# Joint stage and end of a two-layer MetaFormer kernel: other norm instructions, another transpose, new priorities, another plan of the end

## The chip, the core and the metric

The kernel runs on one core of one Trainium2 chip, in a single launch. The core has a matrix engine (TensorE, PE in the profile, its weight loads PEld), three engines for elementwise work (VectorE or DVE, ScalarE or ACT, GpSimd or POOL), and a queue that issues the transfers (SyncE or SP). Each runs its own instructions in the order in which the program gives them, and waits for the others through semaphores. The metric is the device time of one execution in microseconds (us), the median of three: 1247.04 us, from 1245.08 to 1249.42.

## The reference

An image of 64 x 64 tokens with 96 channels goes through two layers. Cut to what matters here:

```python
x = x + L0_conv_ref(ln_c(x))          # layer 0: scan mixer, depthwise convolution
t = t + ffn(ln_t(t), W1, b1, W2, b2)  # layer 0: MLP in fp8 (5,2) products, fp16 sums
x = x + L1_conv_ref(ln_c(x))          # layer 1: scan mixer, full 3x3 convolution
t = t + ffn(ln_t(t), ...)             # layer 1: MLP
# ffn:   h = relu(q16(q16(q8(x) @ q8(W1).T) + q8(b1)));  y = q16(q16(q8(h) @ q8(W2).T) + q8(b2))
# norms: (v - mean(v)) / sqrt(var(v) + eps), over the 96 channels of a token
# layer 1 mixer, per direction: h = exp(dt*A) * h + dt*u*B;  y += sum over 16 states of h*C
#        four directions (rows, columns, both ways), then * silu(z) @ W_out.T
```

## The kernel before, in words

The 4096 tokens are cut into 8 chunks of 512, kept in the tile `res` as 128 partitions x 4 tokens x 96 channels a chunk. Channels of the layer-1 mixer are cut into 6 groups of 32, and its 16 states into 4 sets of 4, so that 24 passes (group g, set k) fill 128 partitions each.

The run has four parts. Layer 0's mixer comes first. Then comes the **joint stage**, written by `middle`: what is left of layer 0's mixer (`mix0`, four pairs of chunks), its MLP (`mlp0`, eight chunks, with `norm` "b" before it and `norm` "c" after it), and the front of layer 1 (`compose1`, `conv_unit`, `project`) are put together into one order. A pair of chunks goes through `mix0`, `mlp0` and the images that the convolution reads (L1553); a convolution unit waits for the images of its chunks and of their neighbours. The stage ends when the last `project` has given the first step sizes to the scans. Third are the 24 **scan passes** (`scans`, the line L2003 holds every scan), with 16 scans of 2.2 to 2.3 us each, one after the other on VectorE. Fourth is the **end**: the last scans of the last pass, and all of what follows from them: the column sums (L2008), the sum over directions, times C, the fold over states into `acc`, the gate (L2359), the output product (L2367), and the MLP of layer 1 on eight chunks (`late_chunk`).

**What sets the order.** In the joint stage and in the end, no order is written by hand. Operations are added to an `Order` with an engine, an assumed cost in us, what they read and write, and which slot of which kind they need (banks, buffers). `Order.run` then walks a modelled clock: of the operations that could start first, it takes the one with the highest rank, which is the longest modelled path to the end plus a lead. `LEAD` gives leads to the parts of the joint stage, `LATE` to the chunks of the end. The engines then run in that order whatever the real durations are. Other tables say which engine takes which variant: `BY_SUMS` (which quarters of the last pass are summed on PE), `TIMES_POOL`, `ROUND_DVE`, `RELU_ACT`, `BIAS_POOL`, `LAST_POOL`.

**A norm** (`norm`, L1453 to L1475) is seven instructions: a DVE sum, a DVE subtraction of the mean, an ACT square, a second DVE sum, an ACT square root, a DVE reciprocal, a DVE product. In `mlp0` the fp8 result is cast by POOL to bf16 (L1489), transposed by PE (L1493) into half-bank slots, and copied by ACT. The MLP's second bias is added as fp32 to fp16 (L1530).

**The end.** The share of channel group 4 (rows 128 to 160 of W_out) in the layer's output is added for chunks 0 to 3 during the last passes, and for chunks 4 to 7 in the end: two kinds of PE products (L2308, the identity times `res`; L2310, four products of 32 rows) into a bank, and an ACT copy back to `res` (L2319). The quarters a = 0 and 1 go by PE sums, an ACT copy and a POOL product (L2328, L2342, L2344), a = 2 and 3 by a POOL sum and a POOL product (L2348, L2349); the backward row scan's part is multiplied on its own (L2354, on DVE for a = 1 and 2). `late_chunk` norms a chunk by two statistics instructions (L2393), a square root, a reciprocal and four products of one token each (L2401).

Of the kernel before, what the change touches and what calls it, by code (L numbers as in the profile page):

```python
# [124 lines left out]

IN_DVE, OTHERS = (), (15, 9, 9)


BY_SUMS, TIMES_POOL = (0, 1), (0, 3)
ROUND_DVE, RELU_ACT = [(2, 2), (5, 1), (5, 2), (6, 2), (7, 0)], [(0, 1), (2, 1), (5, 0), (7, 1)]  # L130
BIAS_POOL, LAST_POOL = (0, 1, 6), (0, 1, 2, 3)
LATE = (103.0, 38.0, -4.0, -6.0, -9.0, -12.0, -12.0, -13.0)


LEAD = {"compose": -5.0}
LEAD |= {("mix", s): t for s, t in enumerate((275.0, 0.0, -10.0, 10.0))}
LEAD |= {("mlp", s): t for s, t in enumerate((65.0, 50.0, 50.0, -145.0))}
LEAD |= {("conv", 0, 0): -275.0, ("conv", 0, "n"): -80.0, ("conv", 0, 1): -860.0}
LEAD |= {("conv", 4, 0): 115.0, ("conv", 4, "n"): 115.0, ("conv", 4, 1): -70.0}
LEAD |= {("project", 0, 0): 25.0, ("project", 0, 1): -45.0, ("project", 4, 0): 125.0, ("project", 4, 1): -235.0}  # L140


class Order:
# [8 lines left out]
    def __init__(self):  # L152
        self.ops, self.free, self.at, self.lead = [], {}, {}, 0.0

# [38 lines left out]
    def run(self, slack=0.0):  # L193
# [15 lines left out]
        while waiting:  # L209
# [23 lines left out]
            for key, tag in new.items():  # L233
                k = min(range(len(self.free[tag])), key=lambda k: self.free[tag][k][0])
                self.at[key] = self.free[tag].pop(k)[1]
            engines[engine] = t + cost
# [21 lines left out]
class Net:  # L258
# [835 lines left out]
    def middle(self, w, pool):  # L1094
# [27 lines left out]
        slots("bank", pb, 7, [P, CH])  # L1122
        t = pb.tile([P, 2, CH], BF16, tag="half", name="half")
        o.slots("half", [t[:, i] for i in range(2)])
        bp = back.enter_context(tc.tile_pool(name="back0", bufs=1))
        for tag, n, shape, dtype in (
            ("r", 2, [P, 2, 4], F32),
            ("nm", 4, [P, 4, 3 + CD], F32),
            ("ss", 1, [P, 4, CD], F32),
            ("x8", 2, [P, 4, CD], FP8),  # L1130
            ("xb", 2, [P, 4, CD], BF16),
# [6 lines left out]
            slots(tag, bp, n, shape, dtype)  # L1138
        spare = [t.rearrange("p a b -> p (a b)")[:, 0:CH] for t in self.diag]
# [4 lines left out]
        o.free["ss"].append((0.0, self.spare[0][:, 0 : 4 * CD].rearrange("p (j d) -> p j d", j=4)))  # L1144
# [197 lines left out]
    def mix0(self, s):  # L1342
# [92 lines left out]
        for k, c in enumerate(chunks):  # L1435
            o.add("ACT", 0.55, kept(c), r=[("oc", c)], new={("ot", c): "ot"})
            o.add("PE", 0.75, turned(c), r=[("ot", c)], new={("ob", c): "bank"})
            o.add("DVE", 1.15, added(k, c), r=[("ob", c), ("r", s)], w=[("res", c)])

    def norm(self, n, c, eps, to, engine="DVE"):  # L1440
# [5 lines left out]
        def spread(t):  # L1446
            return t.unsqueeze(2).to_broadcast([P, 4, CD])

        hold, m, xc, ss, v, r = ((k, n, c) for k in ("nm", "lm", "xc", "ss", "lv", "lr"))
        key = (to, n, c)  # L1450
        mean, dev, inv = (lambda i=i: at[hold].rearrange("p a b -> p (a b)")[:, 4 * i : 4 * i + 4] for i in range(3))
        mid = lambda: at[hold].rearrange("p a b -> p (a b)")[:, 12:].rearrange("p (j d) -> p j d", j=4)
        o.add("DVE", 0.52, lambda: keep(nc.vector.tensor_reduce(mean(), x, AX.X, ALU.add)), r=[("res", c)], new={hold: "nm"}, w=[m])  # L1453
        o.add(
            "DVE",
            0.56,
            lambda: keep(nc.vector.scalar_tensor_tensor(mid(), spread(mean()), -1.0 / CD, x, ALU.mult, ALU.add)),
            r=[m, hold, ("res", c)],
            w=[xc],
        )  # L1460
        o.add("ACT", 0.48, lambda: keep(nc.scalar.activation(at[ss], mid(), AF.Square)), r=[xc, hold], new={ss: "ss"})
        o.add("DVE", 0.52, lambda: keep(nc.vector.tensor_reduce(dev(), at[ss], AX.X, ALU.add)), r=[ss, hold], w=[v])
        o.add(
            "ACT",
            0.27,
            lambda: keep(nc.scalar.activation(dev(), dev(), AF.Sqrt, bias=eps, scale=1.0 / CD)),
            r=[hold],
            w=[v],
            table="sqrt",
        )  # L1470
        o.add("DVE", 0.17, lambda: keep(nc.vector.reciprocal(inv(), dev())), r=[v, hold], w=[r])
        o.add(
            "DVE",
            0.53,
            lambda: keep(nc.vector.tensor_tensor(at[key], mid(), spread(inv()), ALU.mult, saturate=False)),  # L1475
            r=[xc, r, hold],
            new={key: to},
        )
        return key

    def mlp0(self, c):
# [6 lines left out]
        xb, xt = ("xb", c), ("xt", c)  # L1488
        o.add("POOL", 0.6, lambda: keep(nc.gpsimd.tensor_copy(at[xb], at[x8])), r=[x8], new={xb: "xb"})  # L1489

        def turned():
            for j in range(4):
                keep(nc.tensor.transpose(at["t", c][0:CD, j * P : (j + 1) * P], at[xb][:, j, :], self.identb))  # L1493

        o.add("PE", 0.45, turned, r=[xb], new={("t", c): "half"})
        o.add("ACT", 0.55, lambda: keep(nc.scalar.copy(at[xt], at["t", c][0:CD])), r=[("t", c)], new={xt: "xt"})

# [6 lines left out]
        def relu(m):  # L1504
            h, b = ("h16", c, m), b1[:, m : m + 1]
            if m == 0:
                return lambda: keep(nc.scalar.activation(at[h], at[h], AF.Relu, bias=b))
# [5 lines left out]
        for m in range(nm):  # L1513
            o.add("PE", 0.45, up(m), r=[xt], new={("h", c, m): "bank", **({} if m else {("h8", c): "h8"})})
            o.add("ACT", 0.52, rounded(m), r=[("h", c, m)], new={("h16", c, m): "h16"})
            o.add(*(("DVE", 0.42), ("ACT", 0.65))[m == 0], relu(m), w=[("h16", c, m)])
            o.add("POOL", 0.65, small(m), r=[("h16", c, m), ("h8", c)], w=[("h8", c, m)])
# [1043 lines left out]
```

## Time and profile before

The profiled execution took 1247.49 us; its span from the first to the last instruction is 1245.7 us.

| | |
|---|---|
| median of three runs | 1247.04 us |
| profiled execution, its span | 1247.49 us, 1245.7 us |
| busy share of the span: DVE, PE, ACT, POOL | 92%, 82%, 71%, 68% |
| joint stage, from its first product to the first column scan | 104.5 to 319.5 us |
| scan passes | 319.5 to 1161.6 us |
| end, to the last VectorE instruction | 1161.6 to 1242.6 us |

In the rows of groups, the columns are: line, engine, operation, output and inputs by the program's names with their shapes, the number of instructions, their busy time in us, the mean of one in ns, and after the second bar the idle time of the engine just before them and what ended it. In the rows of windows the columns are: the stretch in us from the span's start, its length, busy time and number of instructions of each engine, the granted TensorE clock (1.00 is full), the share of the transfer engines and GB/s. A timeline row gives start, duration, engine, line, operation, and in brackets the idle time before it and its releaser.

### The profile page before, as it was taken

What the parts mean: (1) busy time and instruction counts of PE and PEld (TensorE: products, weight loads), DVE (VectorE), ACT (ScalarE), POOL (GpSimd) and SP (SyncE); (2) the same over time, 40 slices, a digit from 0 to 9 for tenths busy, and PEclk for the clock granted to TensorE, in tenths of its full rate; (3) what the DMA queues carried; (4) which work ended last, traced back from release to release, by engine and by line L of the source; (5) the groups of instructions that cost most, each with busy time, mean ns of one, the idle gap of its engine ahead of it and who ended that gap; (6) DMA issues with size and microseconds to landing.
All of it is one profiled execution on the core that took longest, in us unless ns stands there. A gap on an engine that the chain in (4) does not pass through costs nothing.

```text
span 1245.7 us, 11134 instructions
## 1 busy us (share of the span) xinstructions
PE 1025.0 (82%) x3478; PEld 417.4 (34%) x3478; DVE 1146.2 (92%) x928; ACT 886.1 (71%) x1073; POOL 849.4 (68%) x517
## 2 busy tenths in 40 slices
PE   9997899995287877787977777888778889898887
PEld 5532333331032222233322222233223444344444
DVE  7894987568989999999999999999999999999788
ACT  5582755456587878787887878788778878887535
POOL 3002665323588878888798788978888888876666
PEclk9998989896588788888888879898789999988885
DMA  2252011246844574555734575545736766432301
GB/s 75 75 163 52 1 26 43 85 164 226 271 141 139 179 253 152 178 184 184 244 96 144 203 247 175 173 129 180 238 120 199 239 189 240 148 100 75 99 1 51
DMA packets 79133, 183.15 MB, mean 147 GB/s; under 512 B 21534, under 2 KB 34936, under 8 KB 77688
## 3 DMA queue, kind: packets, MB, share of 16 engines
q1 hardware_dynamic: 78376, 182.16, 46.4%
q8 instruction: 29, 0.48, 0.2%
q14 instruction: 40, 0.33, 0.1%
q10 hardware_dynamic: 688, 0.19, 0.1%
HBM read 159.73 MB, written 21.52 MB: 145 GB/s over the span
## 4 chain that ended last, share of the span: by engine, by line
DVE 42%; PE 14%; issue 9%; ACT 6%; DMA 3%; POOL 0%; another core or an unknown queue 0%; POOLq 0%; DVEq 0%; SPq 0%; ACTq 0%
DVE h1s L2003 13%; DVE xws L2003 12%; DVE h0s L2003 7%; PE hs L2014 6%; DVE x2s L2003 3%; PE hs L2018 3%; DVE x1s L2003 3%; ACT da L1988 2%; DMA kept<-xn 2%; ACT xws L1973 2%; DVE x0s L2003 2%; PE acc L2042 1%; DMA dt<-hss 1%; DVE x0s L2401 1%; PE late L2310 1%
## 5 line engine op out<-in xcount | busy, mean ns | idle before, releaser
L2031 POOL TENSOR_TENSOR kept<-kept,kept 128x1024 f32<-128x1024 f32 x92 | 217.2, 2360 | 81.8 <-issue 40.5
L2008 POOL TENSOR_TENSOR hss<-h1s,xws 128x1024 f32<-128x1024 f32 x96 | 228.1, 2378 | 60.9 <-DVE xws L2003 57.1
L2014 PE MATMUL hs<-h0s,ident 128*128 128x512 f32 x360 | 223.3, 706 | 28.7 <-DVE h0s L2003 24.2
L1988 ACT ACTIVATE da<-dt1s,a 128x1024 f32<-128x1024 f32 x168 | 187.4, 1116 | 70.5 <-DVE xws L2003 55.0
L2003 DVE TENSOR_TENSOR_SCAN xws<-da,xws 128x1024 f32<-128x1024 f32 x96 | 222.9, 2321 | 10.6 <-ACT da L1988 10.3
L1988 ACT ACTIVATE da<-dt0s,a 128x1024 f32<-128x1024 f32 x166 | 185.1, 1115 | 40.7 <-DVE h0s L2003 16.9
L2018 PE MATMUL hs<-hss,ident 128*128 128x512 f32 x368 | 187.7, 602 | 13.9 <-POOL hss L2008 13.8
L2003 DVE TENSOR_TENSOR_SCAN h1s<-da,h1s,xws 128x1024 f32<-128x1024 f32 x72 | 168.0, 2334 | 0.3
L2042 PE MATMUL acc<-kept,fold 128*32 128x512 f32 x368 | 87.8, 689 | 69.5 <-POOL kept L2031 69.5
L2027 ACT COPY kept<-hs 128x512 f32<-128x512 f32 x184 | 106.9, 581 | 46.1 <-PE hs L2018 45.2
L2014 PEld LDWEIGHTS hs<-h0s,ident 128*128 128x128 f32 x360 | 72.9, 220 | 155.8 <-issue 83.0
L2018 PEld LDWEIGHTS hs<-hss,ident 128*128 128x128 f32 x368 | 69.7, 193 | 112.9 <-issue 79.2
L2014 PE MATMUL hs<-x0s,ident 128*128 128x512 f32 x128 | 75.1, 672 | 13.2 <-DVE x0s L2003 13.2
L2014 PE MATMUL hs<-x1s,ident 128*128 128x512 f32 x128 | 74.8, 670 | 12.2 <-DVE x1s L2003 12.2
L2014 PE MATMUL hs<-x2s,ident 128*128 128x512 f32 x120 | 70.2, 670 | 14.6 <-DVE x2s L2003 14.6
L1967 POOL TENSOR_TENSOR x1s<-x1s,dus 128x1024 f32<-128x1024 f32 x32 | 75.7, 2367 | 8.9 <-DMA x1s<-bc 8.9
L1967 POOL TENSOR_TENSOR x2s<-x2s,dus 128x1024 f32<-128x1024 f32 x32 | 75.8, 2370 | 0.4 <-DMA x2s<-bc 0.4
L2003 DVE TENSOR_TENSOR_SCAN x0s<-da,x0s 128x1024 f32<-128x1024 f32 x32 | 74.2, 2320 | 1.7 <-ACT da L1988 1.7
L2003 DVE TENSOR_TENSOR_SCAN x1s<-da,x1s 128x1024 f32<-128x1024 f32 x32 | 74.2, 2320 | 1.7 <-ACT da L1988 1.7
L2003 DVE TENSOR_TENSOR_SCAN x2s<-da,x2s 128x1024 f32<-128x1024 f32 x32 | 74.3, 2322 | 1.1 <-ACT da L1988 1.0
L1973 ACT COPY xws<-x1s 128x1024 f32<-128x1024 f32 x32 | 63.1, 1972 | 5.2 <-POOL hss L2008 5.2
L1967 POOL TENSOR_TENSOR x0s<-x0s,dus 128x1024 f32<-128x1024 f32 x28 | 66.4, 2371 | 0.0
(371 smaller groups left out, 1922.6 us busy)
## 6 DMA issues: line engine op xcount, KB each, us to landing
kept<-bc SPq DMA_DIRECT2D x92, 512.0 KB
x2s<-bc SPq DMA_DIRECT2D x32, 512.0 KB
x0s<-bc SPq DMA_DIRECT2D x28, 512.0 KB
x1s<-bc SPq DMA_DIRECT2D x28, 512.0 KB
dus<-du SPq DMA_DIRECT2D x20, 512.0 KB
dt1s<-dt SPq DMA_DIRECT2D x20, 512.0 KB
dt0s<-dt SPq DMA_DIRECT2D x20, 512.0 KB
kept<-xn SPq DMA_DIRECT2D x24, 384.0 KB
```

The source lines that it names most:

```text
L1967: keep(nc.gpsimd.tensor_tensor(x, x, du[:, part[j]], ALU.mult))
L1973: keep(copy(grid(xw)[:, w, :], cols(xs[i % 3])[:, w, :]))
L1988: keep(nc.scalar.activation(t, dts[o][:, part[j]], AF.Exp, scale=self.a6[:, g, k : k + 1]))
L2003: keep(nc.vector.tensor_tensor_scan(to, da, x, start, ALU.mult, ALU.add))
L2008: keep(nc.gpsimd.tensor_tensor(cols(hs)[:, w, :], grid(h1)[:, w, :], grid(xw)[:, w, :], ALU.add))
L2014: keep(nc.tensor.matmul(t, self.ident, x[:, chunk(m)], start=k == 0, stop=False))
L2018: keep(nc.tensor.matmul(sums[i, m], self.ident, hs[:, chunk(m)], start=False, stop=True))
L2027: keep(nc.scalar.copy(to, sums.pop((i, j * (SC // CH) + h))))
L2031: keep(nc.gpsimd.tensor_tensor(t, t, times_c_by(i, a), ALU.mult))
L2042: keep(nc.tensor.matmul(to, self.fold4, src, start=k == 0, stop=k == NK - 1))
L2310: keep(nc.tensor.matmul(o[:, j], y[:, j:CH:4], w, start=False, stop=j == 3))
L2401: keep(dve.tensor_scalar(at[x8][:, j], x[:, j], at[st][:, j, 1:2], at[sd][:, j : j + 1], ALU.subtract, ALU.mult, saturate=False))
```

## The change

In the **joint stage**, `norm` uses two statistics instructions on pairs of tokens (means and sums of squared deviations come from them), a subtraction, a square root, a reciprocal and a product: the square on ACT and both sums are gone. `mlp0` transposes the fp8 result by products with an fp8 identity (`narrow`), so POOL's cast is gone; its second bias is held in fp16. The eighth bank replaces the two half-bank slots. Ten products of the identity with itself stand ahead of the stage's first product. `LEAD` has other values, and some assumed costs are raised.

In the **end**, the products for group 4 of chunks 4 to 7 no longer go through `res`: with weights laid out in blocks for two chunks (`blocks`), they are summed into the same bank as those of group 5 (`blocked`), and one DVE addition puts both into `res` (`added`). The fourth load of `ye` moves from the end to the scan passes. Only a = 0 goes by PE sums, now with the backward scan's part in it and one DVE product; a = 1 goes as a = 2 and 3 do, and POOL multiplies the backward part of a = 2 and 3. `late_chunk` norms by a subtraction and a product, and chunk 1 by four ACT instructions. `fill` puts products without use into the gaps that the plan leaves on PE. The tables and `LATE` have other values.

```diff
-BY_SUMS, TIMES_POOL = (0, 1), (0, 3)
-ROUND_DVE, RELU_ACT = [(2, 2), (5, 1), (5, 2), (6, 2), (7, 0)], [(0, 1), (2, 1), (5, 0), (7, 1)]
-BIAS_POOL, LAST_POOL = (0, 1, 6), (0, 1, 2, 3)
-LATE = (103.0, 38.0, -4.0, -6.0, -9.0, -12.0, -12.0, -13.0)
-LEAD = {"compose": -5.0}
-LEAD |= {("mix", s): t for s, t in enumerate((275.0, 0.0, -10.0, 10.0))}
-LEAD |= {("mlp", s): t for s, t in enumerate((65.0, 50.0, 50.0, -145.0))}
+BY_SUMS, TIMES_POOL = (0,), (0, 2, 3)
+ROUND_DVE = ((0, 0), (0, 1), (1, 1), (3, 1), (6, 1), )
+RELU_ACT = ((0, 1), (1, 1), (1, 2), (4, 0), (4, 2), (5, 2), (6, 1), (7, 1), )
+NORM_ACT, BIAS_POOL, LAST_POOL = (1,), (0, 1), (0, 1, 2, 4)
+LATE = (195.0, 601.0, -262.0, -558.0, 321.0, -603.0, -581.0, 1149.0)
+LEAD = {"compose": -84.0}
+LEAD |= {("mix", s): t for s, t in enumerate((1589.0, 1847.0, -1582.0, -1562.0))}
+LEAD |= {("mlp", s): t for s, t in enumerate((1510.0, 80.0, 777.0, -2488.0))}
+LEAD |= {("conv", 0, 0): 702.0, ("conv", 0, "n"): 2071.0, ("conv", 0, 1): -2872.0}
+LEAD |= {("conv", 4, 0): -611.0, ("conv", 4, "n"): 13.0, ("conv", 4, 1): -2041.0}
+LEAD |= {("project", 0, 0): -579.0, ("project", 0, 1): -3064.0, ("project", 4, 0): 470.0, ("project", 4, 1): -3512.0}
...
+            if self.fill and engine == "PE":
+                self.fill(t - engines.get(engine, t))
...
-        slots("bank", pb, 7, [P, CH])
+        slots("bank", pb, 8, [P, CH])
+        for _ in range(10):
+            self.keep(nc.tensor.matmul(o.free["bank"][0][1][:, 0:P], self.ident, self.ident, start=True, stop=True))
...
+        def stats():
+            for k in range(2):
+                pair = at[hold].rearrange("p a b -> p (a b)")[:, 6 * k : 6 * k + 6]
+                keep(nc.vector.bn_stats(pair, x[:, 2 * k : 2 * k + 2].rearrange("p j d -> p d j")))
+        o.add("DVE", 0.7, stats, r=[("res", c)], new={hold: "nm"})
+        o.add("DVE", 0.72, lambda: keep(nc.vector.tensor_tensor(mid(), x, spread(st(1)), ALU.subtract)), ...)
+        o.add("ACT", 0.3, lambda: keep(nc.scalar.activation(st(2), st(2), AF.Sqrt, bias=eps, scale=1.0 / CD)), ...)
+        o.add("DVE", 0.17, lambda: keep(nc.vector.reciprocal(st(0), st(2))), ...)
+        o.add("DVE", 0.62, lambda: keep(nc.vector.tensor_tensor(at[key], mid(), spread(st(0)), ALU.mult, saturate=False)), ...)
...
-        o.add("POOL", 0.6, lambda: keep(nc.gpsimd.tensor_copy(at[xb], at[x8])), r=[x8], new={xb: "xb"})
-                keep(nc.tensor.transpose(at["t", c][0:CD, j * P : (j + 1) * P], at[xb][:, j, :], self.identb))
+                keep(nc.tensor.matmul(at["t", c][0:CD, j * P : (j + 1) * P], at[x8][:, j], self.narrow0, start=True, stop=True))
...
-            pairs += [(1, i, k) for i, k in ((n - 3, 2), (n - 2, 2), (n - 1, 3)) for k in range(k)]
+            pairs += [(1, i, k) for i, k in ((n - 3, 2), (n - 2, 2), (n - 1, 4)) for k in range(k)]
...
+            def fill(gap):
+                for _ in range(int(gap * 0.7 / 0.17)):
+                    keep(nc.tensor.matmul(unread[:, 0:HID], self.identb[0:CD], w1, start=True, stop=True))
...
+            for f, t in enumerate(blocks):
+                od.add("POOL", 0.5, lambda t=t: keep(pool.memset(t, 0.0)), w=[("blocks", f)])
+                for q in range(NQ):
...
+                    od.add("ACT", 0.27, lambda t=t, r=r, to=to, src=src: keep(act.copy(t[r, to], src[r])), w=[("blocks", f)])
...
-            for m in range(4, NCH):
-                if m == 7:
-                    od.add("SP", 0.65, lambda: load_y(1, 7), w=[("ye", 1)], kb=64)
-                od.add("PE", 1.6, early(m), r=[("ye", m % 3)], new={("eo", m): "bank"})
-                od.add("ACT", 0.46, lambda m=m: keep(act.copy(self.res[:, m], ...)), r=[("eo", m)], w=[("res", m)])
...
+            def blocked(key, y, w, r, first, end):
+                def f():
+                    for k in range(2):
+                        o = at[key, k][:, 0 : 4 * CD].rearrange("p (j e) -> p j e", j=2)
+                        for j in range(2):
+                            keep(nc.tensor.matmul(o[:, j], y[r, 2 * k + j : CH : 4], w[r], start=first and j == 0, stop=end and j == 1))
...
+                        od.add("PE", 0.95, summed(a, h, h0, True, False), r=ready[-1:], new={key: "bank"})
+                        od.add("PE", 0.95, summed(a, h, hs, False, False), r=whole, w=[key])
+                        od.add("PE", 0.95, summed(a, h, x, False, True), r=[("S", 0, NS + a)], w=[key])
+                        od.add("DVE", 0.69, lambda ...: keep(dve.tensor_tensor(xp[:, half(h)], at[key], t[:, half(h)], ALU.mult)), ...)
...
-                keep(dve.tensor_scalar(at[x8][:, j], x[:, j], at[st][:, j, 1:2], at[sd][:, j : j + 1], ALU.subtract, ALU.mult, saturate=False))
+                keep(act.activation(at[x8][:, j], x[:, j], AF.Identity, bias=at[st][:, j, 0:1], scale=at[sd][:, j : j + 1], saturate=False))
+        if m in NORM_ACT:
...
+            od.add("DVE", 0.74, lambda: keep(dve.tensor_tensor(at[xc], x, spread(at[st][:, :, 1]), ALU.subtract)), ...)
+            od.add("DVE", 0.57, lambda: keep(dve.tensor_tensor(at[x8], at[xc], spread(at[sd]), ALU.mult, saturate=False)), ...)
```

## The prediction

> **What bounds the kernel now.** I first read the windows of the run's parts, as the shares of the page are means over stages with different limits.
>
> ```profile
> 104.50:124.60 20.10, 19.18 (x47) 5.63 (x48) 7.15 (x18) 7.78 (x12) 7.86 (x9) 0.90 0.36 77
> 124.60:213.50 88.90, 77.02 (x352) 31.45 (x352) 76.66 (x165) 53.97 (x111) 50.01 (x66) 0.90 0.07 14
> 213.50:280.60 67.10, 62.75 (x170) 21.89 (x168) 40.02 (x55) 34.22 (x54) 24.57 (x22) 0.92 0.40 129
> 280.60:319.50 38.90, 21.71 (x36) 6.97 (x36) 35.84 (x46) 24.70 (x37) 12.44 (x9) 0.61 0.70 226
> 319.50:1161.60 842.10, 684.04 (x1770) 264.67 (x1771) 830.25 (x373) 665.32 (x695) 686.71 (x315) 0.87 0.56 179
> 1161.60:1195.10 33.50, 28.75 (x84) 14.72 (x82) 24.68 (x13) 14.63 (x19) 22.42 (x14) 0.85 0.05 19
> 1195.10:1242.60 47.50, 38.61 (x240) 22.47 (x240) 42.34 (x105) 21.99 (x47) 33.66 (x37) 0.67 0.07 26
> ```
>
> The first numbers after the length are PE, PEld, DVE, ACT, POOL. The scan passes (fifth row) hold 842 us at 98.6% of VectorE; the change leaves their instructions alone, so I expect 842 again. It acts on 215 us before and 84 us after them. In the joint stage, a start that waits for PE (first row) is followed by the MLP part, where DVE (76.7 of 88.9) and PE (77.0) are both near full; then PE alone is, with the convolution (62.8 of 67.1); then DVE, with the last projection. In the end DVE is idle for 8.8 us while scans are left (sixth row), then busy for 42.3 of 47.5.
>
> Next, the timeline of the end shows what those idle 8.8 us are.
>
> ```profile
> 1177.69 2.10 PE L2310 MATMUL late<-two,ye 32*128 32x96 f32 x8
> ...
> 1179.83 0.48 ACT L2319 COPY res<-late 128x384 f32<-128x384 f32 x1 [2.39 <-PE late L2310]
> 1180.20 2.16 ACT L1988 ACTIVATE da<-dt0s,a 128x1024 f32<-128x1024 f32 x2
> 1181.36 2.35 DVE L2003 TENSOR_TENSOR_SCAN h0s<-da,h0s,x2s 128x1024 f32<-128x1024 f32 x1 [5.29 <-ACT da L1988]
> ```
>
> The copy L2319 waits for PE's products for chunk 7. The decay (L1988) that the next scan needs stands behind that copy in ACT's order, and so the scan starts 5.29 us late. At 1171.27 the same happens with the copy of an earlier chunk: 2.05 us. In the chain that ended last this stretch reads PE L2310, ACT L2319, ACT L1988, DVE L2003.
>
> Last, the groups that the change touches, and their nearest relatives.
>
> ```profile
> L1453 DVE TENSOR_REDUCE nm<-res 128x4 f32<-128x384 f32 x16 | 8.6, 543 | 0.1
> L1457 DVE SCALAR_TENSOR_TENSOR nm<-nm,res 128x384 f32<-128x384 f32 x16 | 13.6, 857 | 0.1
> L1530 DVE TENSOR_TENSOR o<-o,b 128x384 f16<-128x384 f16 x8 | 4.8, 604 | 3.1 <-ACT o L1534 3.1
> L480 DVE TENSOR_TENSOR xna<-res,sta 128x384 f32<-128x384 f32 x8 | 5.2, 648 | 0.0
> L481 DVE TENSOR_TENSOR xna<-xna,sda 128x384 f32<-128x384 f32 x8 | 5.0, 638 | 0.0
> L2393 DVE BATCH_NORM_STATS2 x0s<-res 128x6 f32<-128x192 f32 x16 | 4.7, 347 | 0.0
> L2401 DVE TENSOR_SCALAR x0s<-res,x0s 128x96 fp8e5<-128x96 f32 x32 | 13.5, 482 | 0.1
> L2420 DVE TENSOR_SCALAR x0s<-x0s,b 128x512 f16<-128x512 f16 x20 | 10.1, 530 | 1.2 <-ACT x0s L2416 1.2
> ```
>
> **Joint stage, the norms.** Before, one norm costs DVE 0.543 + 0.857 + 0.545 (L1462, the second sum) + 0.168 (reciprocal) + 0.695 (product, L1475) = 2.81 us. After: two statistics at 0.347, a subtraction, the reciprocal, the product. The subtraction reads two tiles as L1457 does; at that row's 0.857 the norm costs 2.41, at L480's 0.648 it costs 2.20. Sixteen norms save 6.3 to 9.8; I take 7, nearer L1457, which stands in the same place. The second bias goes from 0.604 to the 0.347 of the same addition in fp16 (L2431): 8 x 0.26 = 2.1. DVE loses 9 us. The part's DVE is 86% busy, so I count 0.86 x 9 = **7.8 us** off the path. What takes it over is PE, which needs 77.0 of the 88.9 us: it has 11.9 us idle, enough for 7.8, not for much more. ACT loses 16 squares (L1461) of 0.523, 8.4 us, and POOL 8 casts (L1489) of 0.603, 4.8 us. I count both as nothing, as DVE and PE hide them there (ACT is 54 of 88.9 busy); without that cover, a chain through a norm would be 1.1 us shorter. The fp8 transposes are as many as the bf16 ones; a fp8 one in the end takes 0.316 against 0.227 (L2407, L1493), 32 x 0.09 = 3 us of PE if the clock of the end held here, which those idle 11.9 us cover.
>
> **Joint stage, the ten products ahead.** Each is two rows of a kind that the trace has at 28 in 3.4 us with the clock at 1.00, so 20 take 2.4 us, and 4.8 at the 0.50 that stands here between 104 and 108. All engines leave a branch at 104.5, so nothing hides them, and the means (L1352) are queued behind them, for which DVE and all of `mix0` wait. In return the six means, 4.7 us for the first six rows, run at the full rate's 0.43 each, 2.6. Net **+2.7 us**.
>
> **Joint stage, the order.** Leads of thousands outweigh any path length, so parts follow each other by their leads. The page cannot price this. Bounds: −10 (DVE's 12.2 idle us in the MLP part, nearly all filled) and +12 (one projection more behind the last convolution: three times L1716 to L1725, about 3.3 us of DVE each, in a part where DVE is already 35.8 of 38.9 busy). I take 0. Sum of the stage: **−5 us**, from −15 to +10.
>
> **End, the products for chunks 4 to 7.** Off PE go 4 x (0.84 + 2.03) = 11.5 us, off ACT four copies of 0.48. Back come two `blocked` groups of four products, eight rows each; at L2310's spacing (eight rows in 2.10) 4.2 us of PE, and the same count for group 5 as now (2.1 a quarter). What stood before the decays is gone, so 5.29 + 2.05 = **7.3 us** of DVE idle time go. New on ACT are eight copies of 32 rows, 2.2 us by the plan's own cost, and its decays are 9 of these 33 us: room enough. What is late next is POOL: the last column sum now ends near 1176 instead of 1178.5, then a = 1, 2, 3 need 6 x 2.36 + 4 x 1.27 = 19.2, with six early casts 23: 1199, against 1206.7 now. It moves by the same 7 us. The fourth load of `ye` is one transfer (0.31 us on SP); it goes ahead of the loads of C and of the gate in SP's queue, which has idle stretches of over 15 us there: nothing, and 0.3 us if it had none.
>
> **End, the rest of VectorE.** L2401's 13.5 us become seven chunks of 0.648 + 0.638 = 9.0 and one 0.17 (chunk 1 moves to ACT): −4.3. Four more activations move to ACT (L2420): −2.1. One more bias on DVE: +0.35. The parts of a = 0 and 1 stay four multiplications. Together −6.1; neighbours overlap by some 0.08, so I take **−5**. ACT, 22 of 47.5 busy, gets 4 x 0.735 and four norm products: some 5 us, hidden.
> A rule speaks against the new norm. The Trainium skill ("VectorE: DVE Perf Modes", "The perf-mode tier table") gives one-input fp32 operations two elements a cycle and two-input ones only one; with its fixed 58 cycles ("The TRN2 errata") at 0.96 GHz four products of 96 would cost 0.44 us, two of 384 0.92: 7 x 0.48 = +3.4 instead of −4.3, and my sum would be 1238. The trace has four L2401 in 1.04 us undisturbed, in 4.04 with POOL beside them, and L480 and L481 at 1.29 together. I follow the rows.
>
> **End, the fillers.** The costs in the new plan add up to some 49 us of PE (chunks 8 x 2.74, blocks 11.2, folds 7.7, sums 5.7, rest 2.8). A plan of 70 us leaves 21 of gaps, of which 70% are filled at 0.17 us: 86 products. The skill ("TensorE: Matmul & The Clock Gate", Part 1) has the clock full while PE is busy and halved after an idle window of 3.4 us: by that the fillers hold it, and PE's work shrinks under DVE's. The trace says otherwise:
>
> ```profile
> 1222.00:1228.00 6.00, 5.47 (x35) 3.30 (x34) 6.00 (x17) 3.98 (x9) 4.87 (x8) 0.50 0.10 36
> 1228.00:1234.00 6.00, 5.68 (x29) 2.85 (x28) 5.89 (x16) 4.21 (x8) 4.00 (x6) 0.50 0.16 60
> ```
>
> PE is over 90% busy there at 0.50. At that clock a filler lasts twice as long, 140% of its gap. I take 0: a gain of up to 3 by the rule (a shorter last chunk), a loss of up to 14 by the row.
>
> **Sum.** 1247.5 − 5 − 7.3 − 5 = **1230 us**, against the profiled execution; the median shown is 0.45 lower, within the rounding.
>
> **Rivals.**
> *The joint stage gives nothing* (PE bound, products ahead, or order): PE's 77 of 88.9 speaks for it, its idle 11.9 against it. 1247.5 − 12.3 = 1235.
> *The end's gain is eaten* by fillers at half clock or by POOL (56 of 81 us busy): only about 3 of 12 us stay, 1247.5 − 5 − 3 = 1240; up to 1245.
> *The order is worth 10 more*: 1218.
> *Slower: PE bounds the end.* At 0.50 the work is about 57 us (up products 0.43 for 0.28, folds nearer 1.9 than 1.1); with 21 us of gaps fillers add 29, waits some 4: 90 instead of 81, and 1247.5 − 5 + 9 = 1252. It decides from 18 us of planned gaps on, if the clock is 0.50 all through; the first half of the end at 0.85 speaks against.
> *The change does nothing*, if the removed waits are replaced by others of the same length: 1247.
>
> **Chances.** Forecast 0.52, joint nothing 0.16, gain eaten 0.11 (0.04 of it within the bound), order 0.14, slower 0.05, nothing 0.02. A difference of 0.3% (3.7 us) is about what a measurement of this kernel can tell from none. Faster 0.89, same 0.06, slower 0.05. The forecast's own range is 1222 to 1238; leaving out two in ten, 1214 to 1242.
>
> **What would show it.** L1461, L1462 and L1489 gone; the first scan of the passes near 314 instead of 319.5, and the MLP part some 8 us shorter; the first centring on DVE at about 113 instead of 110.4. In the end, no scan that waits over 1 us for ACT, scans over near 1182 on the new axis (13 us earlier), the last store 17 us earlier. Wrong if the column scans start after 319, if PE is over 95% busy in the end at 0.50, or if POOL's last product comes more than 15 us after the last scan.

## The result, and the profile after

The changed kernel takes 1230.74 us (median of 4 runs, 1229.53 to 1235.15) against 1247.76 us before in the same comparison: a ratio of 0.987, 95% interval 0.984 to 0.990. The forecast was 1230 us. The sum is right; its two parts are not. In the profiled executions (spans of 1245.7 and 1229.9 us) three marks split the run: the start of the first column scan, the start of the last scan, and the end of the span. A time to the end such as 55.5 us counts from the last scan's start; the windows below begin at its end.

| | first column scan | from there to the last scan's start | from there to the end | span |
|---|---|---|---|---|
| before | 319.6 | 873.1 | 53.0 | 1245.7 |
| after | 306.7 | 867.7 | 55.5 | 1229.9 |
| difference, measured | -12.9 | -5.4 | +2.5 | -15.8 |
| difference, forecast | -5 | -7.3 | -5 | -17.3 |

One trace alone is not sharp to a microsecond: kernels with the same old instructions and leads have their first column scan at 318.8 to 321.1 us, kernels with the changed joint stage at 306.1 to 308.1 (five traces).

The windows of the changed kernel, by its own parts (the columns are those of the windows before; the last but two is the granted clock):

```profile
105.00:127.40 22.40, 21.13 (x69) 9.13 (x70) 7.71 (x20) 7.72 (x11) 8.30 (x11) 0.90 0.33 69
127.40:174.20 46.80, 39.22 (x173) 15.17 (x171) 41.17 (x90) 25.58 (x54) 25.97 (x32) 0.93 0.09 18
174.20:215.10 40.90, 40.11 (x196) 17.37 (x196) 29.28 (x75) 22.54 (x43) 19.59 (x30) 1.00 0.08 15
215.10:267.10 52.00, 50.65 (x152) 17.44 (x152) 37.63 (x54) 32.54 (x53) 22.89 (x19) 1.00 0.50 160
267.10:306.70 39.60, 23.66 (x36) 7.17 (x35) 35.62 (x46) 25.11 (x38) 12.94 (x9) 0.58 0.72 226
...
1149.30:1176.70 27.40, 24.08 (x97) 10.41 (x96) 26.45 (x15) 13.08 (x19) 23.53 (x14) 0.94 0.05 19
1176.70:1227.10 50.40, 38.95 (x226) 23.98 (x226) 38.65 (x84) 25.93 (x55) 30.80 (x35) 0.78 0.07 24
```

The MLP part (rows two and three) is not 8 us shorter: the last copy from which images are made (L1541, before L1546) starts at 215.1, before at 213.5. But from 174.2 on PE is busy 40.11 of 40.9 us there, since convolution products already run beside the last MLP groups, and the convolution part behind it takes 52.0 us where it took 67.1. The projections behind the last convolution take 39.6 us, before 38.9. In the end, the scans' part is down from 33.5 to 27.4 us and VectorE is full in it; behind the last scan VectorE is busy 38.65 of 50.4 us, where it was 42.34 of 47.5.

The groups that answer to those shown of before:

```profile
L1471 DVE TENSOR_TENSOR nm<-res,nm 128x384 f32<-128x384 f32 x16 | 12.3, 784 | 0.2
L1468 DVE BATCH_NORM_STATS2 nm<-res 128x6 f32<-128x192 f32 x32 | 9.7, 348 | 0.1
L1525 DVE TENSOR_TENSOR o<-o,bias 128x384 f16<-128x384 f16 x8 | 7.1, 888 | 2.9 <-ACT o L1529 2.9
...
L2417 DVE TENSOR_TENSOR x0s<-res,x0s 128x384 f32<-128x384 f32 x7 | 5.1, 732 | 0.1
L2418 DVE TENSOR_TENSOR x0s<-x0s 128x384 fp8e5<-128x384 f32 x7 | 4.8, 700 | 0.1
L2396 DVE BATCH_NORM_STATS2 x0s<-res 128x6 f32<-128x192 f32 x16 | 4.8, 346 | 0.0
```

The statistics take what they took in the old end, and the subtraction's mean lies between the two rows that the forecast weighed (857 and 648). These means hide two kinds of instruction. The shortest take 0.53 to 0.54 us in each of the three rows (L1457, L480, L1471). All 14 of them that take over 0.7 us end 0.41 or 0.42 us behind the end of a GpSimd instruction: they waited for it, and the means differ by how many did. In the sum of its row the fp16 bias is dearer than the mixed one was (888 for 604 ns). But four of its eight take 0.33 to 0.36 us, as forecast, where the mixed one took 0.54 at least; two, of 1.31 and 3.43 us, make up most of the row.

The timeline where the last scan of the changed kernel ends:

```profile
1174.42 2.33 DVE L1998 TENSOR_TENSOR_SCAN x2s<-da,x2s 128x1024 f32<-128x1024 f32 x1
...
1177.26 0.68 DVE L2357 TENSOR_TENSOR kept<-acc,kept 64x512 f32<-64x512 f32 x1
1178.08 2.35 PE L2287 MATMUL acc<-x2s,fold 128*32 128x512 f32 x4 [1.94 <-DVE kept L2357]
1180.36 5.50 PE L2326 MATMUL da<-x0s,kept 64*128 64x192 f32 x16
1180.47 0.68 DVE L2357 TENSOR_TENSOR kept<-acc,kept 64x512 f32<-64x512 f32 x1 [2.53 <-PE acc L2287]
1183.34 1.02 DVE L2369 TENSOR_TENSOR res<-res,da 128x384 f32<-128x384 f32 x2 [2.19 <-PE da L2326]
```

No scan waits for a copy any more. In its place the gate (L2357) waits 2.53 us for PE's folds, and the addition to `res` (L2369) 2.19 us for the `blocked` products: the first addition comes 6.6 us behind the end of the last scan, before it was 3.9. (The section on the prediction says what PE does in between.)

### The profile page after: what moved, and what is told of

It reads as the page before. It is cut to its first block, busy times and chain, and to the rows that moved or that the text cites. A ratio compares the mean times of both kernels' runs of the same rounds, so it can differ in the third digit from the quotient of the medians.

```text
span 1229.9 us, 11118 instructions
## 1 busy us (share of the span) xinstructions
PE 1013.7 (82%) x3498; PEld 414.7 (34%) x3498; DVE 1134.9 (92%) x908; ACT 881.8 (72%) x1065; POOL 842.4 (68%) x510
## 4 chain that ended last, share of the span: by engine, by line
DVE 46%; issue 11%; PE 10%; ACT 5%; DMA 2%; POOL 1%; SPq 0%; another core or an unknown queue 0%; DVEq 0%; POOLq 0%; ACTq 0%
DVE h1s L1998 14%; DVE xws L1998 13%; DVE h0s L1998 8%; PE hs L2009 4%; DVE x2s L1998 3%; DVE x0s L1998 3%; DVE x1s L1998 3%; PE hs L2013 2%; ACT da L1983 2%; ACT xws L1968 2%; DMA x2s<-bc 1%; PE eo L2123 1%; PE da L2326 1%; POOL hss L2003 1%; DMA kept<-xn 1%
## 5 line engine op out<-in xcount | busy, mean ns | idle before, releaser
L2013 PE MATMUL hs<-hss,ident 128*128 128x512 f32 x368 | 188.1, 603 | 15.4 <-POOL hss L2003 15.3
L1968 ACT COPY xws<-x2s 128x1024 f32<-128x1024 f32 x32 | 63.2, 1976 | 4.2 <-POOL x2s L1962 4.2
```

Source lines behind the costliest of these rows:

```text
L1968: keep(copy(grid(xw)[:, w, :], cols(xs[i % 3])[:, w, :]))
L2013: keep(nc.tensor.matmul(sums[i, m], self.ident, hs[:, chunk(m)], start=False, stop=True))
```

## The experiments

The theory on record was: the norms bring the joint stage's 5 us, the order nothing, the freed scans 7 us of the end and the lighter VectorE 5. The rival after the result: the order brings most of the joint stage's 12.9 us, and in the end a wait takes back what the scans gain. Spans are of the profiled executions; medians and ratios are against before in the same comparison.

**The two halves alone.** First the new joint stage with the old end, then the old joint stage with the new end.

```diff
-BY_SUMS, TIMES_POOL = (0,), (0, 2, 3)
+BY_SUMS, TIMES_POOL = (0, 1), (0, 3)
...
```

> The joint stage of the new kernel with the end of the old one. The recorded split (joint stage 5 us, end 12) gives 1247.5 - 5 = 1242 us, first column scan near 314. The other reading, that the joint stage is worth nearly all of it and the end little, gives 1247.5 - 12.8 = 1235 us, first column scan near 307, end stage still near 81 us.

> The joint stage of the old kernel with the end of the new one. The recorded split gives 1247.5 - 12.3 = 1235 us. If the gain of the end is given back by a wait for PE after the last scan, 1247.5 - 3.2 = 1244 us: end stage near 78 us, VectorE idle for some 11 us after the last scan.

Joint stage alone: 1238.57 us, 0.992 (0.989 to 0.995), first column scan at 306.7. End alone: 1244.96 us, 0.998 (0.997 to 1.000). The second reading holds: the joint stage carries the gain, and the end about 3 us, which its interval can just not tell from nothing. The first is 3.6 us over its 1235, since from the last scan's start to the end it took 55.8 us with the very code that took 53.0 before (see the last section). So the two parts do not simply add: set against this slower form of the old end, the new end is worth 6.8 us by the marks (930.0 to 923.2 from the first column scan on); set against the form of the kernel before, 2.9 (926.1 to 923.2).

**Instructions against order.** One kernel has the new instructions under the old `LEAD`, the other the old instructions under the new `LEAD`.

```diff
-LEAD |= {("mlp", s): t for s, t in enumerate((1510.0, 80.0, 777.0, -2488.0))}
+LEAD |= {("mlp", s): t for s, t in enumerate((65.0, 50.0, 50.0, -145.0))}
...
```

> The new kernel with the old priorities (LEAD) in the joint stage; all new instructions stay. If, as recorded, the order is worth nothing and the statistics instructions bring the joint stage's gain, the time stays at 1231 us and the first column scan at 307. If the new order is what keeps PE full (convolution products beside the MLP's last groups), most of the 12.8 us goes: 1238 to 1243 us, first column scan at 314 to 319, the clock of the MLP part below 1.00 again.

> The old kernel with only the new priorities (LEAD) in the joint stage. By the recorded view the order alone gives 0: 1247 us. If the order is the cause by itself, the first column scan comes 8 to 13 us earlier: 1235 to 1239 us. If order and new instructions only work together (the order is planned on the shorter norms), it gives less than half: 1242 to 1247 us, perhaps slower.

Old leads: 1241.97 us, 0.995 (0.993 to 0.997), first column scan at 316.8. New leads alone: 1241.81 us, 0.995 (0.993 to 0.996), first column scan at 311.3. So the order is worth 8.3 us with the old instructions (319.6 to 311.3) and 10.1 with the new ones (316.8 to 306.7); the instructions are worth 2.8 or 4.6. Of the joint stage's 12.9 us the order is thus 64 to 78%, and clear of the spread of single traces; the instructions' share is not far above that spread. Which of the leads matters was not tried. My expectation that the clock of the MLP part would fall with the old leads was wrong, as the windows up to the last convolution product and behind it show. Before:

```profile
104.50:280.80 176.30, 159.15 (x566) 59.05 (x568) 124.03 (x236) 96.17 (x176) 82.43 (x96) 0.91 0.23 65
```

After:

```profile
105.00:267.30 162.30, 151.31 (x586) 59.17 (x588) 116.00 (x236) 88.58 (x160) 76.75 (x90) 0.97 0.25 70
267.30:306.70 39.40, 23.46 (x36) 7.11 (x32) 35.42 (x46) 24.91 (x37) 12.94 (x9) 0.57 0.72 227
```

New instructions, old leads:

```profile
105.40:268.80 163.40, 151.51 (x584) 59.10 (x584) 117.19 (x236) 88.33 (x160) 79.40 (x90) 0.97 0.25 67
268.80:316.80 48.00, 25.57 (x36) 7.13 (x36) 33.82 (x47) 25.43 (x37) 11.96 (x9) 0.55 0.61 195
```

Old instructions, new leads:

```profile
104.50:271.70 167.20, 150.50 (x566) 57.28 (x568) 121.37 (x236) 94.81 (x176) 80.49 (x96) 0.95 0.25 68
271.70:311.30 39.60, 23.74 (x36) 7.25 (x32) 35.74 (x46) 25.04 (x37) 12.46 (x9) 0.54 0.71 226
```

Up to the last convolution product, each of the two edits alone takes 9 to 13 us off, and the two together 14: PE is busy some 8 us less for the same products, as its clock is 0.95 to 0.97 instead of 0.91. With the new instructions PE is also idle less (11 to 12 us for 17.2), with the new leads alone it is not (16.7). But with the new instructions the old leads lose 8.6 us behind that product, in the last projections. VectorE waits there 15.4 us in all (4.8 in the changed kernel), for the copy that frees a buffer and for ScalarE:

```profile
278.86 0.75 DVE L1712 TENSOR_SCALAR ye<-bank,kept 128x512 f32<-128x512 f32 x1 [3.77 <-POOL hss L1733]
...
303.27 0.75 DVE L1712 TENSOR_SCALAR ye<-bank,kept 128x512 f32<-128x512 f32 x1 [2.00 <-ACT h1s L1711]
306.26 0.43 DVE L1715 TENSOR_SCALAR ye<-h1s 128x512 f32<-128x512 f32 x1 [2.24 <-ACT h1s L1714]
```

With the new leads none of VectorE's waits in that part is over 1.7 us.

**The ten products.**

```diff
-        for _ in range(10):
-            self.keep(nc.tensor.matmul(o.free["bank"][0][1][:, 0:P], self.ident, self.ident, start=True, stop=True))
```

> The new kernel without the ten products ahead of the joint stage. As recorded, they cost 2.7 us net: 1228 us, the first centring on VectorE 5 to 6 us after the branch instead of 8.2, the first column scan near 304. If they pay for themselves by an earlier full clock of TensorE, the first column scan stays at 306.7 and the time at 1231 us.

1230.25 us, 0.984 (0.980 to 0.987); the first centring comes at 110.5 instead of 113.2 and the first column scan at 304.9, 1.8 us earlier. The medians (0.5 us apart) can't tell that from nothing. The traces of three kernels without the ten products can: their first column scan comes at 303.1 to 304.9, that of five with them at 306.1 to 308.1.

**The end: fillers, banks, norms.** Three kernels, each the new one with one thing changed: no `fill`; no `fill` and its bank given to the products from the start; the four products of the old norm.

```diff
-            od.fill = fill
...
-            od.slots("bank", [ph.tile([P, CH], F32, tag="hs", name="late")])
-            unread = ph.tile([P, CH], F32, tag="hs", name="unread")
+            od.slots("bank", [ph.tile([P, CH], F32, tag="hs", name=f"late{i}") for i in range(2)])
...
+                for j in range(4):
+                    keep(dve.tensor_scalar(at[x8][:, j], x[:, j], at[st][:, j, 1:2], at[sd][:, j : j + 1], ALU.subtract, ALU.mult, saturate=False))
```

> The new kernel without the 64 fillers on TensorE in the end; its second bank stays unused. As recorded they are worth nothing: 1231 us. If the fillers hold the clock, the time is up to 3 us longer and the clock of the end falls below 0.83; if they stand before TensorE's work after the last scan, VectorE's 11.8 idle us there shrink and the time is 2 to 5 us shorter, 1226 to 1229 us.

> The new kernel without fillers, and the bank that they wrote to is given to the products of the end from their start. If it is the one bank that makes the sums of a = 0 late (the second half waited for it until after the scans), VectorE's 11.8 idle us after the last scan fall to 5 or 6 and the time to 1225 us. If TensorE's half clock is what makes it late, the idle time stays over 10 us and the time at 1229 to 1231 us.

> The new kernel with the old form of the last norms on VectorE: four products of 96 elements for a chunk in place of a subtraction and a product of 384. By the rows of the old profile (four in 1.93 us beside GpSimd, the pair at 1.43 in the new one) seven chunks cost 3.5 us more: 1234 us. By the page's tier table (0.44 us for four, 0.92 for the pair) they cost 3.4 us less: 1227 us.

*No fillers*: 1233.10 us, 0.986 (0.983 to 0.990). From the last scan's start to the end it takes 57.8 us instead of 55.5 (55.5 to 55.8 in four traces of this end with fillers), and the middle of that stretch runs at a lower clock. The changed kernel, then the one without fillers, from 20 us behind the last scan's end on:

```profile
1196.70:1216.70 20.00, 15.80 (x105) 9.52 (x105) 17.55 (x38) 15.57 (x33) 14.59 (x19) 0.79 0.08 30
```

```profile
1197.50:1217.50 20.00, 15.57 (x89) 9.67 (x88) 15.86 (x35) 14.57 (x31) 13.38 (x18) 0.59 0.05 20
```

PE is busy as long with 16 products fewer, and VectorE gets less done. The fillers earn some 2.3 us by these traces; the medians' ranges overlap.

*Two banks*: 1228.69 us, 0.984 (0.981 to 0.987). The last scan starts 3.0 us sooner behind the first (864.7 for 867.7), as the two products of the sums (L2345, 1.3 us) no longer stand between the scans, and the multiplication that does (L2353) takes 0.67 us where it took 2.57. But VectorE is idle as long in the 20 us behind the last scan (8.7 us for 8.9), and 10.1 for 11.8 us in the whole end behind it, against the expectation of 5 or 6. The 20 us behind the last scan, in the changed kernel and with two banks:

```profile
1176.70:1196.70 20.00, 17.40 (x64) 10.95 (x64) 11.12 (x28) 4.08 (x10) 8.70 (x5) 0.74 0.00 1
```

```profile
1173.10:1193.10 20.00, 19.90 (x74) 9.08 (x74) 11.26 (x25) 4.08 (x9) 13.11 (x9) 0.91 0.00 1
```

PE is busy 19.90 of 20.00 us with both banks, and VectorE 11.3, as with one. The bank was only one of two limits; the other is PE's own work there, of which 5.8 us are the sums of a = 0, which the changed kernel has done before its last scan. PE's half clock is not the whole cause either, as the clock is 0.91 here.

*Four products*: 1235.14 us, 0.989 (0.986 to 0.993), from 1229.5 to 1238.8, too wide to judge by. The profiled execution, the fastest of the five, has this row:

```profile
L2419 DVE TENSOR_SCALAR x0s<-res,x0s 128x96 fp8e5<-128x96 f32 x28 | 10.6, 443 | 0.1
```

10.6 us for seven chunks, where the pair takes 5.1 + 4.8 = 9.9. In this execution neither expectation fits: the new form saves 0.1 us a chunk. The median lies near the first expectation (1234); whether the slower executions pay more for the four products isn't shown.

**The hold-up of the scans alone.** The kernel before, with the products that the copies waited for planned at their real length.

```diff
-                od.add("PE", 1.6, early(m), r=[("ye", m % 3)], new={("eo", m): "bank"})
+                od.add("PE", 2.9, early(m), r=[("ye", m % 3)], new={("eo", m): "bank"})
```

> The kernel before with one number of its plan changed: the products for chunks 4 to 7 (L2310) are planned at 2.9 us of TensorE, as they take in the trace, instead of 1.6. The wait of the scans for ScalarE should go without any other part of the change. If that wait alone is worth what was recorded, the time is 1247.5 - 7.3 = 1240 us. If TensorE's work after the last scan takes most of it back, the last scan comes 5 to 7 us earlier and the time is 1243 to 1247 us.

1245.19 us, 0.998 (0.996 to 0.999). The last scan starts 5.5 us sooner behind the first (867.6 us, as in the changed kernel), but from there to the end it takes 56.2 us, 3.2 longer. What took it back was not the freed PE work, as I had expected: the kernel with the old end behind the new joint stage, whose scans are not freed, takes 55.8 there. Both have a collision on VectorE (last section): here three multiplications that took 1.88 us before take 6.21.

**Combinations.** Without the ten products, with two banks, and with fillers only behind the scans; then the same with 24 warming products ahead of the branch; last without any fillers.

```diff
+                    if end:
+                        unread.append(halves.pop())
...
+        for _ in range(24):
+            keep(nc.tensor.matmul(warm[:, 0:P], self.ident, self.ident, start=True, stop=True))
```

> A combination: the new kernel without the ten products ahead, with both banks for the end's products from their start, and with fillers only after the scans, into a half of the last decay tile. The gains seen singly (1.8 for the ten products by the first column scan, 2 for the banks, the fillers' 2.3 kept) would add up to 1231 - 4 = 1227 us or, if the fillers' share comes on top of the two-bank form, 1225. If TensorE is the bound for the 20 us after the last scan, as it is in the two-bank form (12.90 of 13.0 us busy at clock 1.00), fillers in the plan's gaps there only take its time, and it stays at 1228 to 1230 us.

> As the combination, with 24 warming products placed ahead of the branch, behind the load of its condition, where TensorE idles from 99.3 to 105.0 us. If they fill that idle time, the six means run at the full clock and the first centring is 2 us earlier than without them: 1225 us. If TensorE reaches the branch later for them, by 24 products at 0.13 us, the stage starts up to 3 us later: 1230 us.

> The new kernel without the ten products ahead of the joint stage, with no fillers, and with both banks for the end's products from their start: the two changes that gained singly (1.8 us by the first column scan, and 2.0 us by the medians), together. If they add, 1227 us, the first column scan near 304.5, the last one 66 us later than in the new kernel's own distance less 3. If the fillers' loss (2.3 us) or a lower clock at the stage's start is hidden in them, 1229 to 1231 us, no different from the new kernel.

(In the last one, what was meant is a last scan 3 us sooner behind the first one.)

*With late fillers*: 1234.78 us, 0.991 (0.988 to 0.994): slower than either form alone, with 65.0 us from the last scan's start to the end. The 47 fillers take PE 12.9 us where it has none to give:

```profile
L2307 PE MATMUL da<-w,identb 96*128 96x384 bf16 x47 | 12.9, 383 | 4.1 <-ACT x0s L2435 2.9 <-DVE x0s L2435 0.6 <-ACT x1s L2449 0.6
```

This form also keeps back half a tile that the products had as a bank, so the fillers' share alone isn't shown.

*Warming ahead of the branch*: 1237.27 us, 0.992 (0.989 to 0.995). The 24 products took 7.12 us, and PE left the branch at 108.8 instead of 105.0 (the profiled execution is the slowest of its six):

```profile
99.69 7.12 PE L868 MATMUL warm<-ident 128*128 128x128 f32 x48 [0.33 <-DVE y L877]
108.84 4.51 PE L1363 MATMUL bank<-y,mean 128*128 128x512 f32 x6 [2.04 <-PEq L317]
```

*Two banks, no ten products, no fillers*: 1225.31 us (1224.17 to 1227.31), 0.983 (0.979 to 0.987). It beats the kernel before. Its six runs also lie below the four of the changed kernel, but these were measured in another comparison and the two intervals overlap, so that it beats the changed kernel too is likely and not shown. First column scan at 303.4 (3.3 us earlier), last scan 863.7 behind it (4.0 less), 56.0 to the end.

## Why the prediction was right in its sum and wrong in its parts

That the sum came out is luck: the joint stage gave some 8 us more than forecast, the end some 9 less, and nothing ties the two errors together.

- **Joint stage, the norms: right.** One norm costs 2 x 0.348 + 0.784 + 0.163 + 0.66 (mean of 744 and 580 ns) = 2.3 us, forecast 2.41; 16 save 8 us, forecast 7. The bias went the other way in the sum of its row, +2.3 us instead of -2.1, by its two slow instructions. Instructions and ten products together are worth 2.8 or 4.6 us, forecast 5.
- **The ten products: right.** +2.7 was forecast; the first centring comes 2.8 us later (110.4 to 113.2; 0.5 of it is the branch, left at 105.0 for 104.5), and without them the first column scan comes 1.8 us earlier.
- **The order: the term of the sum that was mis-sized.** "I take 0", between -10 and +12; it measured -8.3 and -10.1. The place was wrong too: I looked for VectorE's idle time in the MLP part, but it lay in PE up to the last convolution product, and, with the new instructions, in the order of the last projections. "It has 11.9 us idle, enough for 7.8, not for much more" took PE's busy time as fixed. It fell by 7.8 us, as the granted clock was 0.97 instead of 0.91: busy time times clock is 145 and 147 us. What lowers the clock is shown only in part. The kernel before has one fall behind idle gaps of PE, and a later one with none:

```profile
148.00:152.00 4.00, 2.22 (x17) 0.94 (x15) 4.00 (x9) 2.50 (x6) 3.39 (x5) 1.00 0.00 0
152.00:156.00 4.00, 2.07 (x10) 1.13 (x6) 3.97 (x11) 3.30 (x8) 2.78 (x5) 0.59 0.01 2
156.00:160.00 4.00, 4.00 (x17) 1.70 (x16) 4.00 (x8) 1.32 (x3) 3.20 (x4) 0.50 0.23 49
160.00:164.00 4.00, 4.00 (x11) 1.43 (x10) 2.58 (x7) 1.44 (x4) 0.41 (x1) 0.50 0.00 0
...
224.00:228.00 4.00, 4.00 (x13) 1.17 (x12) 1.73 (x3) 2.67 (x6) 0.00 (x0) 0.98 0.20 33
228.00:232.00 4.00, 4.00 (x8) 1.21 (x8) 1.60 (x4) 4.00 (x8) 0.00 (x0) 0.59 0.00 0
```

  PE is half idle for 8 us, and then busy all the time at half clock for 8 more. At 228 the clock falls behind windows in which PE was busy throughout. With the new leads alone PE idles as long in sum as before and keeps 0.95, so the sum of the gaps doesn't decide.
- **Sums of the record that don't come out.** With -5 and a bound of +12 for the order, the stage's range ends at +7, not at +10; three times 3.3 us is 9.9, where the bound has 12; and an order worth 10 more gives 1220, not 1218. The forecast of 1230 rests on none of them.
- **End, the hold-up of the scans: the mechanism right, the size 5.4 for 7.3.** VectorE is 26.45 of 27.4 us busy in the scans' part, and no scan there waits over 1 us for ACT. What is missing is new work on VectorE between the last scans: two products of the sums, 1.3 us, and a multiplication that takes 2.57 us there (before 1.52). The two-bank form wins 3.0 us by having neither at that price.
- **"What is late next is POOL ... It moves by the same 7 us": this step failed.** POOL's last product ends at 1185.5, 8.8 us behind the last scan (before 11.7). What is late next is PE, whose work behind the last scan the forecast put on no path. VectorE is idle 8.9 of the 20 us there, before 2.6. Between the last scan and the first additions stand folds and group-5 products, not those of group 4. The folds (L2287) take 2.35 us, before 1.05 (L2278); the group-5 products (L2326, with `kept`) take 5.50 for two quarters, before 2.11 for one (L2367):

```profile
1195.78 1.05 PE L2278 MATMUL acc<-kept,fold 128*32 128x512 f32 x4 [1.47 <-DVE kept L2359]
...
1196.77 2.11 PE L2367 MATMUL da<-two,kept 32*128 32x96 f32 x16
```

  The group-4 products of chunks 4 to 7 cost 4.4 us, as costed (4.2). One half of them is done before the last scan ends, the other stands ahead of a fold for which the gate waits 2.15 us:

```profile
1172.96 2.18 PE L2326 MATMUL da<-x0s,ye 64*128 64x192 f32 x8
...
1188.64 1.25 PE L2326 MATMUL late<-x0s,ye 64*128 64x192 f32 x4
...
1189.73 1.09 PE L2326 MATMUL da<-x0s,ye 64*128 64x192 f32 x4
1190.76 1.05 PE L2287 MATMUL acc<-x2s,fold 128*32 128x512 f32 x4
1191.88 0.69 DVE L2357 TENSOR_TENSOR kept<-acc,kept 64x512 f32<-64x512 f32 x1 [2.15 <-PE acc L2287]
```

  A part of PE's time there is its clock. The first 10 us behind the last scan, in the kernel before, in the changed one, and in the one with four products, whose code is that of the changed kernel up to its norms:

```profile
1195.10:1205.10 10.00, 8.49 (x62) 5.30 (x64) 7.77 (x14) 0.60 (x2) 10.00 (x5) 0.95 0.01 2
```

```profile
1176.70:1186.70 10.00, 8.62 (x24) 5.60 (x26) 4.27 (x10) 0.30 (x1) 8.70 (x5) 0.55 0.01 2
```

```profile
1174.50:1184.50 10.00, 8.68 (x34) 5.76 (x35) 6.44 (x19) 1.67 (x6) 8.73 (x5) 1.00 0.01 2
```

  At full clock the first addition comes 5.0 us behind the last scan instead of 6.6, and VectorE is idle 7.6 of the 20 us instead of 8.9. So of the 6.3 us of new idle time about 1.3 are the clock's, and why it fell in one trace and not in the other isn't shown (it fell at this place in four further traces of this end). That the rest is PE's work is read from the waits and from the two-bank run; a form with fewer products there was not tried.
- **End, the rest of VectorE: the work came off, the time didn't.** By the windows behind the last scan, VectorE's busy time fell by 3.7 us (42.34 to 38.65, forecast 5), and its idle time rose by 6.6 (5.2 to 11.8): +2.9 to its last instruction, +2.5 by the marks. Against the slower form of the old end (55.8 us) the marks give -0.3.
- **The two rules weighed.** On the norm I followed the row (-4.3) against the rule of the Trainium skill ("VectorE: DVE Perf Modes", the tier table; +3.4). The new end saved 1.93 - 1.41 = 0.5 us a chunk against the old kernel; but in the new surroundings the old form costs only 1.51. So neither held. The row's price was that of its neighbour on GpSimd: undisturbed, four products take 1.04 us and a pair 1.00 (L2417 and L2418 from 1188.65 on). The rule's 0.44 us was not reached; the section of its 58 cycles ("The TRN2 errata", on the same page) says itself that some 150 were measured, and with these the estimate is 0.83 for four and 1.11 for a pair. On the fillers I followed the row ("I take 0", a loss of up to 14) against the skill's "TensorE: Matmul & The Clock Gate", Part 1, from which I had a gain of up to 3. The rule came nearer: 64 fillers, not 86, kept the middle of the end at 0.79 instead of 0.59 and earned some 2.3 us.
- **The rivals.** The joint stage's "order worth 10 more" and "the end's gain is eaten" both came true in the main, and cancelled: 1247.5 - 12.9 - 2.9 = 1231.7 by the marks.

## To carry to other kernels

When one engine's wait is removed, ask of every other engine what it still has to do behind that point, PE with its banks first: here half of the five microseconds of freed scans was lost again in waits for PE's folds and products, in part at half clock. PE's busy time isn't fixed, as its clock isn't: another order took 8 us off it for the same products, so an order can't be put at nothing. A price read from the mean of a row is that of its neighbourhood: look at the single instructions, and at what ran beside the slow ones.

## What was not expected of the hardware

- **The same collision can be paid by either engine.** In the kernel before, three multiplications on VectorE (L2354) and a product of twice their length on GpSimd (L2349) meet behind the last scan. Before:

```profile
1195.56 1.88 DVE L2354 TENSOR_TENSOR x2s<-x2s,dus 128x512 f32<-128x512 f32 x3
...
1195.12 4.53 POOL L2349 TENSOR_TENSOR hss<-hss,dus 128x1024 f32<-128x1024 f32 x1
```

  With only the planned cost changed (the same pair of lines):

```profile
1189.92 6.21 DVE L2354 TENSOR_TENSOR x2s<-x2s,dus 128x512 f32<-128x512 f32 x3
...
1190.03 2.79 POOL L2349 TENSOR_TENSOR hss<-hss,dus 128x1024 f32<-128x1024 f32 x1
```

  Once GpSimd pays 2.2 us, once VectorE 4.3. The single instructions show how. Before, VectorE's three products take 0.67 to 0.68 us each, and GpSimd's ends 2.2 us behind the third. In the other trace the first takes 0.70 us; the second ends 0.55 us behind GpSimd's product and the third 0.54 us behind GpSimd's next one, each after 2.83 us. So one engine waits there for a whole instruction of the other. This agrees with the Trainium skill ("SBUF — State Buffer", section "SBUF: two separate sides"), which says of a VectorE operation with two inputs in SBUF and a GpSimd operation that reads SBUF that the one that starts first holds the shared port for its whole instruction. Why GpSimd, whose record starts 0.44 us ahead of the first of the three, had to let all three pass in the kernel before isn't shown. The new joint stage with the old end shows the second form too (6.23 us), the new leads with the old end the first. From the last scan's start to the end the first form goes with 53.0 and 52.9 us, the second with 55.8 and 56.2.
- **Products behind the load of a branch's condition delay the branch.** 24 products in idle time cost 3.8 us at the stage's start, by one trace. PE was idle for the 2.0 us between them and the means, and the six means took 4.51 us, no less than without any warming (4.24 to 4.65 in three traces).
